# A 3x3 convolution by transformed tiles: from 2x2 outputs with 16 resident weight positions to 2x4 outputs with six streamed weight sets

## The chip, the cores and the metric

The kernel runs on one core of a Trainium2 chip, in one launch. The metric is device microseconds (us) of that core. A core has a matrix engine (TensorE, PE in the profile, with its weight loads apart as PEld), a vector engine (VectorE, DVE), an activation engine (ScalarE, ACT), a general engine (GpSimd, POOL), and a queue engine that only issues transfers here (SyncE, SP). Each engine works through its own instructions in order; semaphores tie them together. All arithmetic is in 32-bit floating point.

## What is computed

Two images of 256 channels and 64x64 pixels go through two layers, each added to its input. Layer 0 is an eight-head self-attention over all 4096 pixels. Layer 1 normalises by groups of channels, makes q, k and v by 1x1 products, and returns the mean of two branches: two block-wise attentions one after the other ("long range" over blocks, then "short range" inside blocks of 8x8, called `sr` below), and a 3x3 convolution over fixed mixtures of q, k and v:

```python
f_all = jnp.einsum('bidn,oi->bodn', jnp.concatenate([qh, kh, vh], 1), fc_w)
f_conv = f_all.transpose(0, 2, 1, 3).reshape(b, hd * KC * KC, h, w)
out_conv = lax.conv_general_dilated(f_conv, dep_w, (1, 1), ((1, 1), (1, 1)), feature_group_count=hd, dimension_numbers=('NCHW', 'OIHW', 'NCHW'))
return rate1 * out_att + rate2 * out_conv
...
x = x + _L0_conv_ref(_gn(x), L0_conv_qkv_w, L0_conv_qkv_b, 8)
x = x + _L1_conv_ref(_gn(x), ...)
```

Since everything before the convolution is linear, the kernel folds `conv1_w`, `conv2_w`, `conv3_w`, `fc_w` and `dep_w` into one dense 3x3 convolution with 256 input and 256 output channels. The change concerns how this convolution is done.

## The kernel before

**Stages.** Each image goes through five: statistics and projections of layer 0; its attention (TensorE, VectorE and ScalarE in an order written out by hand); `layer1_first`, which is the first attention of layer 1; and `layer1_second`, which holds the second attention and the convolution. Image 0 ends before image 1 begins, but for loads and statistics of image 1 that are worked in at the end (`following`). A second program, `general_layers`, is in the file for inputs whose softmax sums leave a safe range; it does not run here.

**Tiles.** A picture is held in eight tiles `xts[t]` of 128 partitions by 2 (channel halves) by 512 pixels (8 rows). `xp` is the normalised picture with a border of zeros. Working tiles come from one pool of 12 places (tag `w4`, 4 KB a partition): the hidden layers, v, z, `res` and others share it. A tile can be written when the last reader of the tile that had its place is done.

**The convolution before.** It uses the transform for 2x2 outputs from 4x4 inputs: 16 products stand for the 36 of the direct form. The picture is cut into four strips `s` of 16 rows, and each strip is worked in four steps, one for each column position `q`; a step handles all four row positions `r`. So an image has 16 steps, the two images 32. In one step:

- `conv_transform` (GpSimd): one operation makes `col` (1152 elements a partition) from strided columns of `xp` (L972), then four make the row positions, 512 elements each, in two `v` tiles (L976). It is called for the step after the one that is about to run.
- `conv_step`, products (TensorE, L986): 4 row positions x 2 output halves x 2 input halves, each 128x128 by 256 columns, into one PSUM tile `mm` of four banks, of which there is only one.
- `conv_step`, the way back: ScalarE copies one row position out of PSUM (L991), VectorE combines the others to two output rows in `z` (L992 to L995), and then adds or subtracts z into every second column of x: operations with the bias on 128 elements (L1007), the rest on 256 (L1011, L1013).

**Weights.** `conv_weights` (VectorE) folds them for one half `m` of the channels at a time: nine taps by twelve scaled additions (L905, L907), four row combinations, and from each row four column positions (L916 to L918), sent to DRAM in pieces of 128 KB by SyncE (L920). It runs while image 0's first attention tiles are worked. `fetch_conv_weights` loads all 16 positions (4 MB) to one place of 32 KB a partition (tag `vw`), which layer 0 uses for its values. For image 0 it also turns them on TensorE, 64 transposes through PSUM (L945), scales them on VectorE and ScalarE on the way back (L950, L948), and stores the turned ones to DRAM (L951) for image 1, which only loads them.

**The order in `layer1_second`.** It loops over eight tiles t of the second attention. Each has two branches of two layers of products with ScalarE evictions (`branch`, q then k: L1339, L1348), values, scores, a softmax on VectorE and ScalarE (L1084 to L1091), a transpose of it (L1096, `at`), copies (L1105) and the weighted sum (L1114). TensorE's order is that of the program text; the other engines' is set by a planner. `spots` says at which of three places in a tile a step is put: 0 between the branches, 1 between the softmax's start and its transpose, 2 at the tile's end. `images` says when the tiles of `xp` are made (`to_image`, ScalarE; before the loop also VectorE). `give(n)` adds the attention's result `res` to `xts[n]` and stores it once the strip that holds n is complete; `following` loads image 1 into the places of x that have become free.

```python
spots = {t: (0, 1, 2) for t in range(2, 7)} | {7: (0,)} if b == 0 else {
    t: (0, 1, 2) if t < 2 else (0, 1) for t in range(NT - 1)
}
```

Of the kernel before, what the change touches and what calls it, by code (L numbers as in the profile page):

```python
# [9 lines left out]
F32 = mybir.dt.float32  # L10
# [30 lines left out]
def direct_layers(ctx: ExitStack, tc: tile.TileContext, a: dict, out: bass.AP, bad: bass.AP):  # L41
# [805 lines left out]
    def conv_weights():  # L847
# [7 lines left out]
        prep, rest = place[:, :n_prep], place[:, n_prep : n_prep + 27 * C].rearrange("p (i c) -> p i c", c=C)  # L855
        wx, taps, new_rows = rest[:, 0:12], rest[:, 12:21], rest[:, 21:27]
        new_cols = rest[:, 0:8].rearrange("p (r j) c -> p r j c", j=2)
# [39 lines left out]
        for m in range(2):  # L897
# [16 lines left out]
            for r, row in enumerate((g[0], one, two, g[2])):  # L914
                one, two = new_cols[:, r, 0, :], new_cols[:, r, 1, :]
                nc.vector.tensor_add(one, row[:, 0, :], row[:, 2, :])  # L916
                nc.vector.tensor_sub(two, one, row[:, 1, :])
                kept["made"] = nc.vector.tensor_add(one, one, row[:, 1, :])  # L918
                for q, src in enumerate((row[:, 0, :], one, two, row[:, 2, :])):
                    nc.sync.dma_start(  # L920
                        out=wf_kept[:, :, 4 * r + q, m * P : (m + 1) * P], in_=src.rearrange("p (k c) -> p k c", k=KC)
                    )
# [6 lines left out]
    UW = 16  # L929
    wf_kept = dram.tile([P, KC, UW, C], F32, name="wf_kept")  # L930

    def fetch_conv_weights(b):

        wf = vpool.tile([P, KC, UW, C], F32, tag="vw", name=f"wf_{b}")
        for r in range(4):
            nc.sync.dma_start(out=wf[:, :, 4 * r : 4 * r + 4, :], in_=wf_kept[:, :, 4 * r : 4 * r + 4, :])
        if b > 0:
            return wf
        for pos in range(UW):
            r, q = divmod(pos, 4)  # L940
            pw = bank([P, KC, C], f"pw_{pos}")
            for k in range(KC):
                for m in range(2):
                    block = slice(m * P, (m + 1) * P)
                    nc.tensor.transpose(pw[:, k, block], wf[:, k, pos, block], ident)  # L945
            scale = (0.5 if r in (1, 2) else 1.0) * (0.5 if q in (1, 2) else 1.0)
            if pos % 2:
                nc.scalar.activation(wf[:, :, pos, :], pw, AF.Copy, scale=scale)  # L948
            else:
                nc.vector.tensor_scalar(wf[:, :, pos, :], pw, scale, None, ALU.mult)  # L950
        nc.sync.dma_start(out=wf_kept, in_=wf)  # L951
        return wf
# [6 lines left out]
    STRIP = 8 * (W // 2)  # L959

    def conv_transform(b, xp, s, q):

        def cols(d):
            return xp[:, :, 16 * s : 16 * s + 18, d : d + W - 1 : 2]

        def rows(d):
            return col[:, :, d : d + 15 : 2, :]

        terms = ((0, 2, False), (1, 2, True), (2, 1, False), (1, 3, False))
        col = cpool.tile([P, KC, 18, W // 2], F32, tag="col", name=f"col_{b}_{s}_{q}")  # L970
        one, two, plus = terms[q]
        (nc.gpsimd.tensor_add if plus else nc.gpsimd.tensor_sub)(col, cols(one), cols(two))  # L972
        v = [w4([P, 2, KC, STRIP], f"v_{b}_{s}_{q}_{n}") for n in range(2)]
        for r, (one, two, plus) in enumerate(terms):
            dst = v[r // 2][:, r % 2].rearrange("p k (i j) -> p k i j", j=W // 2)
            (nc.gpsimd.tensor_add if plus else nc.gpsimd.tensor_sub)(dst, rows(one), rows(two))  # L976
        return v

    def conv_step(b, xts, wf, v, s, q, pacc):


        mm = pacc.tile([P, 2, 4, STRIP], F32, tag="acc", name=f"mm_{b}_{s}_{q}")
        for r in range(4):
            for m in range(2):
                for k in range(KC):
                    nc.tensor.matmul(  # L986
                        mm[:, m, r, :], wf[:, k, 4 * r + q, m * P : (m + 1) * P], v[r // 2][:, r % 2, k, :],
                        start=k == 0, stop=k == KC - 1,
                    )
        z = w4([P, 2, 2, STRIP], f"z_{b}_{s}_{q}")  # L990
        nc.scalar.copy(z[:, 1], mm[:, :, 1, :])  # L991
        nc.vector.tensor_add(z[:, 0], z[:, 1], mm[:, :, 0, :])  # L992
        nc.vector.tensor_add(z[:, 0], z[:, 0], mm[:, :, 2, :])
        nc.vector.tensor_sub(z[:, 1], z[:, 1], mm[:, :, 2, :])
        nc.vector.tensor_sub(z[:, 1], z[:, 1], mm[:, :, 3, :])  # L995
        bias = kept["bias"][1]
        for half in range(2):
            xs = xts[2 * s + half].rearrange("p m (i r j c) -> p m i r j c", i=4, r=2, c=2)
            for r in range(2):
                zs = z[:, r, :, half * (STRIP // 2) : (half + 1) * (STRIP // 2)].rearrange(  # L1000
                    "p m (i j) -> p m i j", i=4
                )
                for c in range(2):
                    dst = xs[:, :, :, r, :, c]
                    if q - c == 0:
                        for m in range(2):
                            nc.vector.scalar_tensor_tensor(  # L1007
                                dst[:, m], zs[:, m], bias[:, m, 0:1], dst[:, m], ALU.add, ALU.add
                            )
                    elif (q, c) in ((1, 0), (2, 0)):  # L1010
                        nc.vector.tensor_add(dst, dst, zs)  # L1011
                    elif (q, c) in ((2, 1), (3, 1)):
                        nc.vector.tensor_sub(dst, dst, zs)  # L1013
# [255 lines left out]
    def layer1_second(b, xts, feats, mean, rstd, shift, pacc, following):  # L1269
# [8 lines left out]
        def to_image(t, both=False):  # L1278
# [10 lines left out]
        results = {}  # L1289
        turns = [divmod(n, 4) for n in range(4 * NT // 2)]  # L1290
# [5 lines left out]
        spots = {t: (0, 1, 2) for t in range(2, 7)} | {7: (0,)} if b == 0 else {  # L1296
            t: (0, 1, 2) if t < 2 else (0, 1) for t in range(NT - 1)
        }
        images = {1: range(5), 3: (5, 6), 4: (7,)} if b == 0 else {0: (3, 4), 1: (5,), 2: (6,), 3: (7,)}

        def conv():
            nonlocal done, wf
            if wf is None:
                wf = fetch_conv_weights(b)
            if done + 1 < len(turns):
                ahead[done + 1] = conv_transform(b, xp, *turns[done + 1])
            conv_step(b, xts, wf, ahead.pop(done), *turns[done], pacc)
            done += 1

        def give(n):  # L1310
            res = results.pop(n)
            halves = out[b, :, n * T : (n + 1) * T].rearrange("(k p) n -> p k n", p=P)
# [9 lines left out]

        if b:
            with tc.issue_after(kept["feats"].ins):
                for t in range(3):
                    to_image(t, True)
            ahead[0] = conv_transform(b, xp, *turns[0])
        pending, then = None, following()
        for t in range(NT):
# [25 lines left out]
            with tc.manual_schedule(engines={mybir.EngineType.PE}):  # L1355
# [9 lines left out]
                if b == 0 and t == NT - 1:  # L1365
                    for n in sorted(results):
                        give(n)
# [44 lines left out]
            for n in sorted(n for n in results if done >= 4 * (n // 2 + 1)):  # L1412
                give(n)
# [599 lines left out]
```

## Time and profile before

| what | us |
|---|---|
| three runs | 3078.77, 3077.24, 3078.86 (median 3078.77) |
| the profiled execution, its own time | 3078.72 |
| its span, first to last instruction | 3076.7 |
| `layer1_second`, image 0 | about 1256 to 1561 |
| `layer1_second`, image 1 | about 2784 to the end |
| products of the convolution (L986), busy | 227.6 |
| GpSimd, v of the transform (L976), busy | 165.4 |
| GpSimd, col of the transform (L972), busy | 69.5 |
| VectorE, updates of x (L1007; L1011; L1013) | 69.3; 28.9; 32.1 |

In the profile a line of instructions has its start, its length, the engine, the line of the program, the operation, what is written and read, the shape, and in brackets how long the engine had been idle before and what ended that. A matmul of 32-bit numbers appears as two, so a step's 16 products are counted as 32. The granted clock is TensorE's, 1.00 at full rate. Lines of transfers on SPq show when they were issued, not when they landed.

### The profile page before, as it was taken

To read this page: it belongs to the slowest core of one execution; us is meant where nothing else is said; L and a number is where in the kernel's file an instruction comes from. 1 tells how busy PE (TensorE), PEld (TensorE's weight loads), DVE (VectorE), ACT (ScalarE), POOL (GpSimd) and SP (SyncE) were. 2 spreads that over 40 slices of the span, in tenths; PEclk is the share of its full clock that TensorE was granted. 3 is DMA by queue.
4 is the path that set the end of the run, shared out by engine and by line. 5 is a ranking of instruction groups with operands and counts; after the bars stand their busy time and mean duration, and the time that the engine had idled before them with its cause. 6 is when DMAs were issued, how large, how long until landed. Compare 5 with 4: busy or idle time off the path is not lost. (4 is left out here: it accounts for less than half of the span.)

```text
span 3076.7 us, 63947 instructions
## 1 busy us (share of the span) xinstructions
PE 2991.9 (97%) x25129; PEld 1865.1 (61%) x25129; DVE 2455.0 (80%) x3122; ACT 2339.2 (76%) x3262; POOL 837.5 (27%) x923
## 2 busy tenths in 40 slices
PE   6999999999999999999989999999999999999998
PEld 3555556655556656577755556566555565576765
DVE  4598999999899989856556989989989899835543
ACT  2699999999999984622237999999999999734333
POOL 2032222322223230055301222222222222306440
PEclk9999999999999999999999999999999999999999
DMA  7979679787897661230159787897888976700000
GB/s 241 270 142 185 146 157 173 156 176 150 171 182 163 141 133 33 76 137 28 41 191 268 137 169 164 159 179 150 169 166 166 182 153 128 169 4 4 21 14 22
DMA packets 243795, 424.48 MB, mean 138 GB/s; under 512 B 99112, under 2 KB 109916, under 8 KB 241308
## 3 DMA queue, kind: packets, MB, share of 16 engines
q0 software_dynamic: 94992, 238.36, 40.3%
q1 hardware_dynamic: 147580, 181.68, 21.8%
q8 instruction: 199, 3.26, 0.4%
q14 instruction: 112, 0.92, 0.1%
q10 hardware_dynamic: 912, 0.27, 0.0%
HBM read 119.03 MB, written 68.39 MB: 61 GB/s over the span
## 5 line engine op out<-in xcount | busy, mean ns | idle before, releaser
L541 ACT ACTIVATE es<-ring 128x512 f32<-128x512 f32 (+2 forms) x1572 | 1204.1, 908 | 31.7 <-PE ring L535 23.7
L535 PE MATMUL ring<-q,k 128*128 128x512 f32 x4096 | 1085.0, 408 | 11.4 <-ACT v L541 6.2
L587 DVE TENSOR_TENSOR e<-e,es 128x1024 f32<-128x1024 f32 (+1 forms) x956 | 1035.7, 1145 | 23.7 <-ACT es L541 23.3
L535 PEld LDWEIGHTS ring<-q,k 128*128 128x128 f32 x4096 | 734.5, 188 | 383.2 <-ACT es L541 114.8
L541 ACT ACTIVATE v<-ring 128x512 f32<-128x512 f32 (+2 forms) x1024 | 781.2, 903 | 25.6 <-PE ring L535 12.9
L550 PE MATMUL av<-es,v 128*32 128x256 f32 (+1 forms) x9684 | 725.8, 389 | 0.0
L587 DVE TENSOR_TENSOR e<-e,v 128x1024 f32<-128x1024 f32 (+1 forms) x636 | 669.8, 1109 | 25.2 <-ACT v L541 24.2
L550 PE MATMUL av<-v 128*32 128x256 f32 (+1 forms) x6188 | 498.4, 389 | 0.0
L550 PEld LDWEIGHTS av<-es,v 128*32 128x32 f32 x9684 | 328.1, 110 | 265.9 <-issue 106.4
L550 PEld LDWEIGHTS av<-v 128*32 128x32 f32 x6188 | 221.5, 110 | 170.8 <-issue 72.3
L986 PE MATMUL mm<-v,wf 128*128 128x256 f32 x1024 | 227.6, 380 | 1.5 <-DVE z L995 1.5
L597 POOL DMA_DIRECT2D es<-es x118 | 100.7, 853 | 462.1 <-ACT es L541 392.4
L986 PEld LDWEIGHTS mm<-v,wf 128*128 128x128 f32 x1024 | 193.3, 190 | 36.8 <-issue 9.8
L976 POOL TENSOR_TENSOR v<-col 128x512 f32<-128x512 f32 x128 | 165.4, 1318 | 178.4 <-ACT rk_sr L1127 39.9
L991 ACT COPY z<-mm 128x512 f32<-128x512 f32 x32 | 18.7, 585 | 183.3 <-PE mm L986 183.3
L597 POOL DMA_DIRECT2D acc<-es x118 | 117.6, 1002 | 122.7 <-ACT es L541 43.0
L595 POOL DMA_DIRECT2D es<-es x20 | 11.4, 568 | 505.1 <-ACT es L541 414.8
L597 POOL DMA_DIRECT2D es<-v x72 | 61.3, 852 | 294.8 <-ACT v L541 288.7
L992 DVE TENSOR_TENSOR z<-z,mm 128x512 f32<-128x512 f32 x32 | 22.0, 687 | 139.7 <-ACT z L991 139.3
L597 POOL DMA_DIRECT2D v<-es x112 | 116.7, 1042 | 19.6 <-ACT es L541 10.2
L597 POOL DMA_DIRECT2D acc<-v x78 | 76.2, 977 | 75.9 <-ACT es L541 28.5
L972 POOL TENSOR_TENSOR col<-xp 128x1152 f32<-128x1152 f32 x32 | 69.5, 2173 | 62.4 <-DVE xp L1405 51.0
(252 smaller groups left out, 2685.8 us busy)
## 6 DMA issues: line engine op xcount, KB each, us to landing
acc<-es POOLq DMA_DIRECT2D x128, 512.0 KB, 6.4
acc<-v POOLq DMA_DIRECT2D x84, 512.0 KB, 6.1
es<-es POOLq DMA_DIRECT2D x138, 256.0 KB, 4.3
v<-es POOLq DMA_DIRECT2D x132, 256.0 KB, 5.2
k<-wk_halves SPq DMA_DIRECT2D x64, 512.0 KB
q<-wq_halves SPq DMA_DIRECT2D x256, 128.0 KB
v<-v POOLq DMA_DIRECT2D x90, 256.0 KB, 4.8
es<-v POOLq DMA_DIRECT2D x84, 256.0 KB, 3.9
```

What stands on the lines that cost most here:

```text
L535: touch(nc.tensor.matmul(sc[:, i, :], held["k", g // 2][:, j * P : (j + 1) * P], held["q", g, u // 2][:, u % 2, :], start=True, stop=True, ...
L541: nc.scalar.activation(dst, sc, AF.Exp, scale=SC0), set(range(at % BANKS, at % BANKS + m))
L550: note(nc.tensor.matmul(dst[HD0 * u : HD0 * u + HD0, n], lhs, rhs(u)[:, n], start=start, stop=stop))
L587: nc.vector.tensor_add(dst[:, s, :], dst[:, s, :], src)
L595: nc.gpsimd.dma_start(out=dst, in_=src)
L597: nc.gpsimd.dma_start(out=dst, in_=src, accum_op=ALU.add)
L972: (nc.gpsimd.tensor_add if plus else nc.gpsimd.tensor_sub)(col, cols(one), cols(two))
L976: (nc.gpsimd.tensor_add if plus else nc.gpsimd.tensor_sub)(dst, rows(one), rows(two))
L986: nc.tensor.matmul(mm[:, m, r, :], wf[:, k, 4 * r + q, m * P : (m + 1) * P], v[r // 2][:, r % 2, k, :], start=k == 0, stop=k == KC - 1,)
L991: nc.scalar.copy(z[:, 1], mm[:, :, 1, :])
L992: nc.vector.tensor_add(z[:, 0], z[:, 1], mm[:, :, 0, :])
```

## The change

The convolution's transform becomes one of two output rows by four columns: 4 row positions and six column positions, 24 products for 72.

- The picture is cut into two halves of 32 rows, each worked in six steps (`TURNS`: sets 0 to 5 for the upper half, 5 to 0 for the lower). A step again has 16 products of 256 columns. An image has 12 steps.
- `conv_transform` makes `col` (1088 elements) in four operations: two elementwise ones of GpSimd with a scaling by ScalarE between the first and the second, and a third of GpSimd. The four row operations remain, of 512 elements.
- The way back: z is laid out by picture tile; the bias is added by ScalarE where set 1 is copied out. VectorE then adds z, with a factor of 1, -1, 2, -2, 4, -4, 8 or -8, into every fourth column of each of the four tiles: four operations of 256 elements in sets 0 and 5, sixteen in the others.
- `conv_weights` makes six column positions from each row, with three scaled additions more, and sends 24 pieces for each half of the channels in place of 16.
- A class `ConvWeights` holds four of the six sets (1 MB each) in the same 32 KB a partition. Sets 4 and 5 are loaded after steps 0 and 1 of the upper half, sets 1 and 0 after the lower half's first two steps. For image 0, sets 0 to 3 are turned before the first step, 4 before the second, 5 before the third (96 transposes in all), and each set is stored.
- `spots` and `images` have new entries for 12 steps; before its loop image 1 makes five tiles of `xp` instead of three.
- Results: a tile of which the half is not complete has its attention result added to x (`add_result`) and is later stored from x itself (`give_summed`).

```diff
-        new_cols = rest[:, 0:8].rearrange("p (r j) c -> p r j c", j=2)
+        new_cols = [[rest[:, at, :] for at in range(4 * r, 4 * r + 4)] for r in range(3)]
+        new_cols.append([rest[:, at, :] for at in (15, 16, 17, 27)])
...
+                nc.vector.scalar_tensor_tensor(far[0], row[:, 2, :], 4.0, row[:, 0, :], ALU.mult, ALU.add)
+                nc.vector.scalar_tensor_tensor(far[1], row[:, 1, :], -2.0, far[0], ALU.mult, ALU.add)
+                kept["made"] = nc.vector.scalar_tensor_tensor(
+                    far[0], row[:, 1, :], 2.0, far[0], ALU.mult, ALU.add
+                )
+                for q, src in enumerate((row[:, 0, :], *near, *far, row[:, 2, :])):
...
+    TURNS = [(0, q) for q in range(NQ)] + [(1, q) for q in reversed(range(NQ))]
...
+        def fetch(self, q):
+            nc.sync.dma_start(out=self.wf[:, slot(q)], in_=wf_kept[:, q])
+            if q not in self.whole:
+                self.raw.append(q)
...
+        def used(self, n):
+
+            s, q = TURNS[n]
+            after = {(0, 0): 4, (0, 1): 5, (1, 5): 1, (1, 4): 0}.get((s, q))
+            if after is not None:
+                self.fetch(after)
...
+        (nc.gpsimd.tensor_add if plus else nc.gpsimd.tensor_sub)(col, cols(one), cols(two))
+        nc.scalar.activation(col, col, AF.Copy, scale=by)
+        (nc.gpsimd.tensor_add if third_plus else nc.gpsimd.tensor_sub)(col, col, cols(third))
+        nc.gpsimd.tensor_add(col, col, cols(fourth))
...
+    BY = ((1, 0, 0, 0), (1, 1, 1, 1), (1, -1, 1, -1), (1, 2, 4, 8), (1, -2, 4, -8), (0, 0, 0, 1))
...
+        for t in range(4):
+            xs = xts[4 * s + t].rearrange("p m (a j c) -> p m a j c", j=W // NC, c=NC)
+            zs = z[:, :, t, :].rearrange("p m (a j) -> p m a j", j=W // NC)
+            for c, by in enumerate(BY[q]):
+                dst = xs[:, :, :, :, c]
+                if abs(by) == 1:
+                    kept["given"] = (nc.vector.tensor_add if by > 0 else nc.vector.tensor_sub)(dst, dst, zs)
+                elif by:
+                    kept["given"] = nc.vector.scalar_tensor_tensor(dst, zs, float(by), dst, ALU.mult, ALU.add)
...
-        spots = {t: (0, 1, 2) for t in range(2, 7)} | {7: (0,)} if b == 0 else {
-            t: (0, 1, 2) if t < 2 else (0, 1) for t in range(NT - 1)
+        spots = {2: (0, 1), 3: (0, 1, 2), 4: (0, 1), 5: (0, 1), 6: (0, 1), 7: (0,)} if b == 0 else {
+            0: (1,), 1: (0, 1), 2: (0, 1), 3: (0, 1), 4: (0, 1), 5: (0, 1), 6: (0,)
         }
-        images = {1: range(5), 3: (5, 6), 4: (7,)} if b == 0 else {0: (3, 4), 1: (5,), 2: (6,), 3: (7,)}
+        images = {1: range(5), 3: (5, 6, 7)} if b == 0 else {0: (5, 6), 1: (7,)}
...
+            wf.turn()
             conv_step(b, xts, wf, ahead.pop(done), *turns[done], pacc)
+            wf.used(done)
...
+        def add_result(n, res):
+
+            for m in range(KC):
+                x = xts[n][:, m, :]
+                nc.vector.scalar_tensor_tensor(x, res[:, m, :], wts["rate1"], x, ALU.mult, ALU.add)
+            summed.append(n)
...
+        def give_summed():
+            for n in [n for n in summed if whole(n)]:
+                nc.sync.dma_start(out=of_image(n), in_=xts[n])
+                summed.remove(n)
...
-                for t in range(3):
+                for t in range(5):
                     to_image(t, True)
```

## The prediction

> **What bounds the kernel now.** I read the engines' shares first, then three windows.
>
> ```profile
> span 3076.7 us, 63947 instructions
> PE 2991.9 (97%) x25129; PEld 1865.1 (61%) x25129; DVE 2455.0 (80%) x3122; ACT 2339.2 (76%) x3262; POOL 837.5 (27%) x923
> ```
>
> ```profile
> 1256.00:1561.00 305.00, 291.22 (x1380) 205.04 (x1379) 196.29 (x405) 109.16 (x189) 121.61 (x85) 0.98 0.18 65
> 1340.00:1350.00 10.00, 7.51 (x34) 5.85 (x34) 8.82 (x23) 3.03 (x5) 1.02 (x2) 0.83 0.01 2
> 2784.00:3070.00 286.00, 280.73 (x1297) 193.92 (x1297) 133.99 (x267) 98.18 (x172) 117.58 (x80) 0.99 0.04 14
> ```
>
> The columns are stretch, length, then PE, PEld, DVE, ACT and POOL busy, the granted clock, DMA share and GB/s. The first and third are the two stages that hold the convolution (image 0, image 1). TensorE is the bound in both (95% and 98%); the others have room on average. The change can gain only by taking work from TensorE, and lose only where it makes TensorE wait. The middle row is such a wait, and TensorE's order of time around it shows the price of a step:
>
> ```profile
> 1315.70 7.15 PE L945 MATMUL pw<-ident,wf 128*128 128x128 f32 x64
> 1322.69 7.07 PE L986 MATMUL mm<-v,wf 128*128 128x256 f32 x32
> 1329.60 1.89 PE L1050 MATMUL pvs_sr<-wt_fv,feats 128*128 128x256 f32 x8
> 1331.42 1.15 PE L1068 MATMUL sp_sr<-rk_sr,rq_sr 128*64 128x64 f32 x32
> 1333.49 7.14 PE L986 MATMUL mm<-v,wf 128*128 128x256 f32 x32 [0.92 <-DVE z L995]
> 1343.12 0.44 PE L1096 MATMUL at_sr<-ident,e_sr 128*128 128x128 f32 x2 [2.49 <-DVE e_sr L1091]
> 1343.40 3.08 PE L1050 MATMUL pvs_sr<-wt_fv,feats 128*128 128x256 f32 x8
> ```
>
> What TensorE waited for there, on VectorE and GpSimd:
>
> ```profile
> 1333.26 7.45 DVE L1007 SCALAR_TENSOR_TENSOR x<-z,edges,x 128x128 f32<-128x128 f32 x7
> 1340.63 0.41 DVE L1084 TENSOR_REDUCE nm_sr<-sp_sr 128x4 f32<-128x256 f32 x1
> ```
>
> ```profile
> 1332.73 5.08 POOL L976 TENSOR_TENSOR v<-col 128x512 f32<-128x512 f32 x4 [5.65 <-PE sp_sr L1068]
> 1337.89 2.14 POOL L972 TENSOR_TENSOR col<-xp 128x1152 f32<-128x1152 f32 x1
> ```
>
> An update of x takes 0.34 us alone (median of L1007), but seven took 7.45 here, because each came through once per GpSimd instruction; the softmax's reduction L1084 stood behind them. This is the hazard of the change.
>
> **Part by part.**
>
> *Products.* A step is 16 products before and after, 256 columns each. It occupies TensorE from 1322.69 to 1329.60, 6.91 us. 32 steps become 24: 8 x 6.91 = **-55.3**.
>
> *Transposes.* 64 took 1315.70 to 1322.69, 0.109 each. 32 more: **+3.5**.
>
> *First step.* The bias leaves VectorE's eight half-size updates; four remain there. The wait above goes: 0.92 + 2.49, plus the slowed matmuls behind (3.08 for 1.89, and 2.57 for the 2.22 us of pc elsewhere, 1.5): **-4.9**.
>
> *GpSimd.* The rows:
>
> ```profile
> L976 POOL TENSOR_TENSOR v<-col 128x512 f32<-128x512 f32 x64 | 83.0, 1321 | 96.5 <-ACT rk_sr L1127 34.1 <-issue 15.0 <-DVE x L1013 14.1
> L972 POOL TENSOR_TENSOR col<-xp 128x1152 f32<-128x1152 f32 x16 | 34.6, 2163 | 10.2 <-ACT xp L1285 9.0
> L1007 DVE SCALAR_TENSOR_TENSOR x<-z,edges,x 128x128 f32<-128x128 f32 x64 | 32.1, 552 | 0.0
> L1011 DVE TENSOR_TENSOR x<-x,z 128x256 f32<-128x256 f32 x32 | 13.4, 418 | 0.0
> ```
>
> Before: 2.16 + 4 x 1.32 = 7.4 us a step. After: three column operations of 1088 elements, 2.08 by interpolating between these two rows, and four of 1.32, 11.5 us; the ScalarE scaling between them I put at 1.4 (between one and two of xp's 0.81 us for 512 elements). A chain of 13 us. A picture tile with two steps lasts 34.8 us (its first product at 2905.57, the next tile's at 2940.35), 17.4 a step, so it hides, with one transform worked ahead; only image 0's tile of three steps is near the limit. **0**; without that cover it costs what exceeds the step's interval.
>
> *VectorE.* Updates now: 128 x 0.344 + 128 x 0.418 = 97 us if alone, 130.3 measured (69.3 + 28.9 + 32.1), so 33 us of blocking, of which 4.9 reached TensorE. After: 72 updates of 256 elements per half picture, 288 in all, 192 adds at 0.418 and 96 scaled at 0.476 (L907's row) = 126 alone. z falls by 8 x 4 x 0.683 = 22. Average load is no bound, but the middle sets give 16 updates to a step, and GpSimd's busy share in the two convolution stretches (214 + 248 = 462 us) rises from 238/462 = 52% to 276/407 = 68%. Blocking scaled by both: 33 x 126/97 x 68/52 = 56; with the share 4.9/33 that reached TensorE, 8. That row has at most 12 updates in a step, so I take twice it, **+16**. Lower bound 0. Upper: in a tile with two such steps all 14 GpSimd instructions (23 us) let one update through each; the 18 other updates cost 7.7, two sums of results 1.5, z 5.5, the softmax and its copies 2.7, together 40.4 against 34.8, 5.6 us late, and 1.5 of slow clock; 16 such steps make 8 such pairs, 57. The wait is for the softmax; at_sr, pvs_sr and pc_sr are queued behind it on TensorE.
>
> *ScalarE's scaling* waits in ScalarE's queue for GpSimd's first subtraction. If placed early, the evictions behind it wait, and TensorE's branch products wait for those. Bounds: 0, and 2.1 + 1.4 less 1.0 of slack in a branch (half of its second layer's 3.6 us of products against an eviction of 0.78), 24 x 2.5 = 60. TensorE's waits for ScalarE in these stretches are a few us in total today, so nearer the low end: **+5**.
>
> *Weights of image 0.*
>
> ```profile
> 1295.65 9.07 SPq L920 DMA_DIRECT2D wf_kept<-prep  x11
> 1306.40 2.65 SPq L936 DMA_DIRECT2D wf<-wf_kept  x4
> ```
>
> Stores are issued 0.66 us apart; 17 instead of 11 come at the end (+4), and VectorE's 9 late extra operations at 0.40 pitch (3.6) lie beside that. The loads start near 1310.4, the transposes are due at 1315.70 and had no wait; I take **+3**, 0 to 12 (the first half's 8 extra stores stand before the loads of the second half).
>
> *Set 4* is loaded after step 0 and transposed before step 1. TensorE has 1.89 + 1.15 = 3.0 us between; today's four loads, issued from 1306.40, had all been used by 1322.69, at most 4.1 us each, and a lone load also has its start-up; I take 5. **+2**, 0 to 7. Set 5 has a whole tile's end and the next branch, 11 us, and image 1's later fetches four steps: 0. SP stands behind these waits, with only result stores and x loads.
>
> *Outputs* come from x itself, so image 1's last three x tiles load only after a store. Before, the stage's end has 16 statistics in VectorE from 1542.31 to 1554.95, which cover most: **+2**, 0 to 6. Image 1's five tiles of picture instead of three are covered since its first step moves one branch and the scores later. Sums of results replace the gives one for one: 0.
>
> Sum: 3076.7 - 55.3 + 3.5 - 4.9 + 16 + 5 + 3 + 2 + 2 = 3048.0. The profiled execution's own time, 3078.72, is 2.0 above its span, and the median 3078.77 equals it: **3050**.
>
> [...] The trace has a 0.83 clock after 2.49 us idle. [...]
> [...]
>
> **Rivals.** (A) The above: 3050, 3030 to 3070, chance 0.48.
> (B) VectorE, ScalarE and the loads hide it all, as TensorE's 98% speaks for: 3078.7 - 55.3 + 3.5 - 4.9 = 3022, chance 0.15. Against it: the wait at 1343.
> (C) The blocking decides: slower from 5.6 us per pair of heavy steps, as (3076.7 - 3032.0)/8; at the upper bound 7.1 it gives 3050 + 57 - 16 = **3091**, slower. For it: 7.45 us for seven updates. Against: 56 of today's 64 L1011 updates met no GpSimd instruction. 0.20.
> (D) ScalarE's queue blocks in each transform: 3050 + 60 - 5 = 3105. Nothing like it in the trace, since no ScalarE instruction there waits for GpSimd. 0.08.
> (E) The weights come late at every place: +12 + 7 + 6 for 7: 3068. 0.09.
>
> **Numbers.** 0.2% (6 us) is about what a measurement here can tell. Faster: A 0.44, B 0.15, E 0.07, 0.66. Same: 0.10 from the edges of A, E and C. Slower: C 0.16, D 0.08, 0.24. Range 3022 to 3094, B to C.
>
> **What would show it.** 768 products of 256 columns in place of 1024 by the trace's count; GpSimd near 11.5 us a step; L1007's successors above 0.42 where GpSimd runs; TensorE's waits at at_sr (my +16), at the branch products (ScalarE), at pw (weights). I am wrong if TensorE's idle time in the two stages grows beyond 50 us, or does not grow at all.

## The result, and the profile after

The changed kernel takes 3148.52 us (median of four runs, 3147.52 to 3150.63) beside 3078.82 (3077.24 to 3079.41) for the kernel before: a ratio of 1.0223, 95% interval 1.021 to 1.0236. It is **slower by 69.7 us**. The prediction said 3050 and gave 3022 to 3094, so it has the wrong sign and the time lies outside its range. One execution of experiment 5 below took 9620.31 us, for 3119.40 to 3121.59 of its three others, and is left out of that experiment's median.

The engines' shares of the profiled execution after:

```profile
span 3148.7 us, 63534 instructions
PE 2969.5 (94%) x24905; PEld 1831.1 (58%) x24905; DVE 2598.6 (83%) x3152; ACT 2360.0 (75%) x3284; POOL 952.0 (30%) x931
```

TensorE has 22.4 us less work (2991.9 before), and the span is 72.0 us longer, so some 94 us of new idle time stand against it. It lies in the two stages. In the names of the profile, `phq_sr` and `phk_sr` are the first-layer products of the q and the k branch in PSUM, `hq_sr` and `hk_sr` ScalarE's evictions of them (copies out of PSUM), `prq_sr`, `prk_sr`, `rq_sr` and `rk_sr` the same of the second layer; `e_sr` is the softmax, `at_sr` its transpose, `bd` the copy of that, `pc_sr` the weighted sum, `pw` the turning of the weights, and `mm` the accumulator of the convolution's products. These are the stretches of image 0 and image 1, each taken from the first `phq_sr` product to the stage's end, and 20 us inside the first (columns as before: stretch, length, PE, PEld, DVE, ACT, POOL busy, granted clock, DMA share, GB/s):

```profile
1262.16:1607.90 345.74, 280.96 (x1268) 190.24 (x1269) 267.56 (x418) 118.51 (x199) 179.64 (x89) 0.91 0.22 78
2829.35:3148.70 319.35, 265.63 (x1169) 173.88 (x1169) 198.15 (x267) 105.74 (x178) 174.87 (x84) 0.93 0.08 27
1436.00:1456.00 20.00, 5.22 (x12) 2.70 (x12) 19.89 (x15) 1.93 (x3) 14.74 (x7) 0.66 0.00 1
```

The stages last 345.7 and 319.4 us, for 302.3 and 292.6 before from and to the same instructions. TensorE's gaps between matmuls, added up in the trace's records (without the last wait of image 0's stage, 3.1 us in both kernels), are 107.1 us in the two, for 12.0 before, and the clock is granted at half for 110.5 us, for 21.8. The clock is the second loss: products and transposes alone were to take 51.8 us from TensorE's work, but only 22.4 us are gone, since the matmuls behind the gaps run slowly (the eight of `prq_sr` behind the longest wait for ScalarE, shown below, took 5.91 us for 3.60 where nothing was late). So the account is -22.4 + 95.1 = +72.7, for 72.0 measured.

What TensorE waited for, from the waits of the whole span (total, times, longest):

```profile
PE prq_sr L1413 <- ACT hq_sr L1172: 41.3, 12, 10.4
...
PE at_sr L1141 <- DVE e_sr L1136: 17.2, 7, 4.6
PE mm L1027 <- DVE z L1049: 14.8, 1, 14.8
PE prk_sr L1413 <- ACT hk_sr L1172: 7.5, 2, 7.0
PE pc_sr L1159 <- ACT rq_sr L1172: 7.2, 1, 7.2
PE pw L970 <- DVE e_sr L1131: 5.1, 1, 5.1
```

Before, the waits for `hq_sr` were not there, and those for `e_sr` were these:

```profile
PE at_sr L1096 <- DVE e_sr L1091: 3.6, 2, 2.5
```

More than half of the new waits are for ScalarE (some 60 of the 95 us), which has more room than TensorE and VectorE; so one has to ask what ScalarE waited for:

```profile
ACT x L1065 <- DVE x L1056: 66.9, 18, 20.9
...
ACT col L1008 <- POOL col L1007: 52.1, 9, 12.6
```

These are the border corrections behind the late updates of x, and the new scaling behind GpSimd's first column operation. The groups of the convolution's own instructions (busy us, mean ns, idle before):

```profile
L1027 PE MATMUL mm<-v,wf 128*128 128x256 f32 x768 | 176.0, 389 | 14.8 <-DVE z L1049 14.8
L1056 DVE TENSOR_TENSOR x<-x,z 128x256 f32<-128x256 f32 x192 | 170.3, 981 | 0.8
...
L1015 POOL TENSOR_TENSOR v<-col 128x512 f32<-128x512 f32 x96 | 136.4, 1451 | 1.9
L1058 DVE SCALAR_TENSOR_TENSOR x<-z,x 128x256 f32<-128x256 f32 x96 | 102.5, 1129 | 0.0
L1009 POOL TENSOR_TENSOR col<-col,xp 128x1088 f32<-128x1088 f32 x24 | 76.0, 3167 | 128.4 <-ACT col L1008 128.4
L1010 POOL TENSOR_TENSOR col<-col,xp 128x1088 f32<-128x1088 f32 x24 | 73.3, 3056 | 1.9
...
L1007 POOL TENSOR_TENSOR col<-xp 128x1088 f32<-128x1088 f32 x24 | 64.5, 2688 | 67.3 <-DVE xp L1469 55.0 <-ACT xp L1330 10.6
```

The updates of x before:

```profile
L1007 DVE SCALAR_TENSOR_TENSOR x<-z,edges,x 128x128 f32<-128x128 f32 x128 | 62.9, 542 | 0.0
L1013 DVE TENSOR_TENSOR x<-x,z 128x256 f32<-128x256 f32 x64 | 30.8, 502 | 0.0
L1011 DVE TENSOR_TENSOR x<-x,z 128x256 f32<-128x256 f32 x64 | 28.9, 451 | 0.0
```

The products fell as predicted, 1024 to 768. The updates of x keep VectorE busy for 170.3 + 102.5 = 272.8 us, for 62.9 + 30.8 + 28.9 = 122.6. (Neighbouring updates overlap a little. By the sum of their lengths, which is what the table ahead of the prediction gives with 130.3, they take 296.8 us.) GpSimd's four kinds take 136.4 + 76.0 + 73.3 + 64.5 = 350.2 us, 14.6 us a step.

**The longest wait, read closely.** VectorE, then GpSimd, then TensorE, in order of time:

```profile
1435.40 8.40 DVE L1058 SCALAR_TENSOR_TENSOR x<-z,x 128x256 f32<-128x256 f32 x3
1443.71 1.70 DVE L1056 TENSOR_TENSOR x<-x,z 128x256 f32<-128x256 f32 x1
1445.26 6.20 DVE L1058 SCALAR_TENSOR_TENSOR x<-z,x 128x256 f32<-128x256 f32 x3
1451.36 0.68 DVE L1046 TENSOR_TENSOR z<-z,mm 128x512 f32<-128x512 f32 x1
```

```profile
1434.63 3.71 POOL L1009 TENSOR_TENSOR col<-col,xp 128x1088 f32<-128x1088 f32 x1 [1.22 <-ACT col L1008]
1438.41 3.31 POOL L1010 TENSOR_TENSOR col<-col,xp 128x1088 f32<-128x1088 f32 x1
1441.80 6.23 POOL L1015 TENSOR_TENSOR v<-col 128x512 f32<-128x512 f32 x4
1448.11 2.86 POOL L1007 TENSOR_TENSOR col<-xp 128x1088 f32<-128x1088 f32 x1
```

```profile
1454.23 2.04 PE L1027 MATMUL mm<-v,wf 128*128 128x256 f32 x4 [14.78 <-DVE z L1049]
```

Seven updates take the 16 us of seven GpSimd instructions, one for each. The four z operations, the last of which releases the accumulator, stand behind them, and the next step's product waited 14.78 us. The row of 1436 to 1456 above shows the price: VectorE 19.89 of 20.00 busy, TensorE 5.22, clock 0.66. The z operations themselves, which have one input in PSUM, all take 0.67 to 0.69 us, also beside GpSimd.

The other kind of wait, in ScalarE's order of time, and TensorE's row:

```profile
1303.27 0.42 ACT L1132 ACTIVATE e_sr<-e_sr 128x256 f32<-128x256 f32 x1 [0.23 <-DVE e_sr L1131]
1313.24 1.11 ACT L1008 ACTIVATE col<-col 128x1088 f32<-128x1088 f32 x1 [9.56 <-POOL col L1007]
1314.26 1.43 ACT L1172 ACTIVATE hq_sr<-phq_sr,vecs 128x512 f32<-128x512 f32 x2
```

```profile
1315.07 5.91 PE L1413 MATMUL prq_sr<-hq_sr,wt_fq 128*128 128x512 f32 x8 [10.44 <-ACT hq_sr L1172]
```

The scaling waited 9.56 us for GpSimd, and the evictions of `hq_sr`, whose products were complete about 1304.6, stood behind it: TensorE's wait of 10.4 us. There GpSimd itself began late, at 1310.32, since the clearing of the picture's border (L1469) is put behind VectorE's preparation of the weights. The kernel before had that order too (its GpSimd began at 1303.21), but nothing on ScalarE stood behind GpSimd.

### The profile page after: what moved, and what is told of

The parts are those of the page before. It is cut to its first block, busy times and chain, and to the rows that moved or that the text cites. A ratio compares the mean times of both kernels' runs of the same rounds, so it can differ in the third digit from the quotient of the medians.

```text
span 3148.7 us, 63534 instructions
## 1 busy us (share of the span) xinstructions
PE 2969.5 (94%) x24905; PEld 1831.1 (58%) x24905; DVE 2598.6 (83%) x3152; ACT 2360.0 (75%) x3284; POOL 952.0 (30%) x931
## 4 chain that ended last, share of the span: by engine, by line
PE 46%; DVE 9%; ACT 2%; POOL 1%; DMA 1%; issue 1%; ACTq 0%; POOLq 0%; DVEq 0%
PE ring L535 16%; PE av L550 14%; PE mm L1027 4%; DVE x L1056 3%; DVE x L1058 3%; PE prq_sr L1413 1%; PE p_wk L406 1%; PE py L1211 1%; PE pvs_lr L1095 1%; PE pv L429 1%; PE p_wq L406 1%; PE prk_sr L1413 1%; PE pvs_sr L1095 1%; PE phk_sr L1404 1%; PE ring L550 1%
## 5 line engine op out<-in xcount | busy, mean ns | idle before, releaser
L1027 PE MATMUL mm<-v,wf 128*128 128x256 f32 x768 | 176.0, 389 | 14.8 <-DVE z L1049 14.8
L1027 PEld LDWEIGHTS mm<-v,wf 128*128 128x128 f32 x768 | 148.6, 195 | 41.2 <-issue 20.4
L1056 DVE TENSOR_TENSOR x<-x,z 128x256 f32<-128x256 f32 x192 | 170.3, 981 | 0.8
L1015 POOL TENSOR_TENSOR v<-col 128x512 f32<-128x512 f32 x96 | 136.4, 1451 | 1.9
L597 POOL DMA_DIRECT2D v<-es x112 | 115.4, 1030 | 17.2 <-ACT es L541 9.0
L1009 POOL TENSOR_TENSOR col<-col,xp 128x1088 f32<-128x1088 f32 x24 | 76.0, 3167 | 128.4 <-ACT col L1008 128.4
L1413 PE MATMUL prq_sr<-hq_sr,wt_fq 128*128 128x512 f32 x128 | 71.8, 705 | 41.4 <-ACT hq_sr L1172 41.3
L1058 DVE SCALAR_TENSOR_TENSOR x<-z,x 128x256 f32<-128x256 f32 x96 | 102.5, 1129 | 0.0
```

The lines of the kernel that those rows point to most:

```text
L597: nc.gpsimd.dma_start(out=dst, in_=src, accum_op=ALU.add)
L1009: (nc.gpsimd.tensor_add if third_plus else nc.gpsimd.tensor_sub)(col, col, cols(third))
L1027: nc.tensor.matmul(mm[:, r, m, :], wf.wf[:, slot(q), k, r, m * P : (m + 1) * P], v[r // 2][:, r % 2, k, :], start=k == 0, stop=k == KC - 1,)
L1056: kept["given"] = (nc.vector.tensor_add if by > 0 else nc.vector.tensor_sub)(dst, dst, zs)
L1058: kept["given"] = nc.vector.scalar_tensor_tensor(dst, zs, float(by), dst, ALU.mult, ALU.add)
L1413: nc.tensor.matmul(pr[m], wts[two][:, k, m * P : (m + 1) * P], hid[:, k, :], start=k == 0, stop=k == KC - 1)
```

## The experiments

Two theories at first. **L**: VectorE's updates are late (each update excludes, and is excluded by, GpSimd's instructions, and costs more alone than I had put down), and everything else is late because of them. **Q**: ScalarE's queue is the cause, by the scaling that waits for GpSimd and the border corrections that wait for updates. All edits are to the changed kernel.

**1. The scaling on GpSimd.**

```
-        nc.scalar.activation(col, col, AF.Copy, scale=by)
+        nc.gpsimd.tensor_scalar(col, col, by, None, ALU.mult)
```

> The changed kernel, with the scaling of col done by GpSimd instead of ScalarE, so that no ScalarE instruction of the convolution waits for GpSimd. Theory Q (ScalarE's queue: evictions stand behind the scaling): the waits of TensorE for the evictions of t=2 of image 0 and t=0 of image 1 (10.4, 7.2, 4.3 and 7.0 us) go, and some slow clock with them: 3105 to 3120. Theory L (VectorE's updates and GpSimd's operations exclude each other, and the rest follows from late updates): GpSimd gets 24 operations more, so 3148 or up to 20 more.

Measured: 3143.72 us, ratio to the kernel before 1.0208 (1.0178 to 1.0238). The waits changed place:

```profile
PE at_sr L1141 <- DVE e_sr L1136: 42.7, 6, 15.5
...
PE prq_sr L1413 <- ACT hq_sr L1172: 28.5, 9, 9.5
```

The waits for the softmax (VectorE) rose from 17.2 to 42.7 as those for ScalarE fell. Q alone falls.

**2. The border corrections left out.**

```
-            for tt in ((), (0, 1))[t] if b == 0 and t < 2 else (t,):
-                conv_edges(xts, tt)
```

> The changed kernel without the border corrections of the bias (conv_edges left out, so border pixels lack them). Theory Q: ScalarE's border operations wait for late updates of x and hold up evictions (5.0, 5.9, 8.9 and 3.4 us at hq); without them 3115 to 3125. Theory L in its strict form (TensorE waits for VectorE itself): within 5 us of 3148.

Measured: 3138.62 us, 1.0191 (1.0162 to 1.0221), 10 us less: between the two expectations, nearer L's.

**3. Both at once.**

> Both of the former: GpSimd scales, and the border corrections are left out. Theory Q: nothing in ScalarE's queue waits for GpSimd or for updates of x any more, so most of the 60 us of waits for evictions go: 3070 to 3090. Theory L strict: 3140 to 3170.

Measured: 3142.17 us, 1.0203 (1.0173 to 1.0233). No wait of note for `hq_sr` is left; those for `e_sr` are 61.2 us, and the time is within 7 us of the changed kernel's. ScalarE's queue was mostly where the lateness showed, not what made it: L.

**4. A third of the updates.** Of sets 0 to 4 only the first column that has a factor is updated: 96 updates for 288.

```
-            for c, by in enumerate(BY[q]):
+            for c, by in enumerate(BY[q][:1] if q < 5 else BY[q]):
```

> The changed kernel with one column of updates a step (96 updates of x in place of 288; three of four columns do not get sets 1 to 4). Theory L: VectorE and GpSimd no longer contend, waits at the softmax and at z and late border operations go: 3070 to 3085. Theory Q with the scaling alone as the cause: the four waits behind the scaling stay (29 us and slow clock), 3110 to 3125.

Measured: 3092.95 us, 1.0045 (1.0025 to 1.0065): 55.6 us less, between the two ranges and nearer L's. L gets most of it, but the waits for `hq_sr` keep 26.0 us (longest 10.4), so the scaling has a price of its own, which experiment 1 could not show while VectorE was late.

**5. z in PSUM.** Does L come from the exclusion (L1 below) or from the price of an update alone (L2)? The two last z operations write to the accumulator's first two banks, whose products are used up by then; the updates then have one SBUF input.

```
-        nc.vector.tensor_add(z0, z0, products(2))
         nc.vector.tensor_sub(z1, z1, products(2))
-        nc.vector.tensor_sub(z1, z1, products(3))
+        zp = mm[:, 0:2].rearrange("p r m s -> p (r m s)").rearrange("p (m t s) -> p m t s", m=2, t=4)
+        of_row = zp.rearrange("p m t (i r j) -> p (m t i) r j", r=2, j=W // NC)
+        nc.vector.tensor_add(of_row[:, :, 0, :], z0, products(2))
+        nc.vector.tensor_sub(of_row[:, :, 1, :], z1, products(3))
...
-            zs = z[:, :, t, :].rearrange("p m (a j) -> p m a j", j=W // NC)
+            zs = zp[:, :, t, :].rearrange("p m (a j) -> p m a j", j=W // NC)
```

> The last two of the four z operations write z into the accumulator's first two banks in PSUM in place of SBUF, so each of the 288 updates of x has one SBUF input and not two; nothing else is changed. Theory L1 (the updates are late because an operation of VectorE with two SBUF inputs and GpSimd's operations exclude each other): no update is over 1 us any more, their mean is 0.63 to 0.75 us (981 and 1129 ns in the changed kernel), their sum 180 to 215 us for 272.8, and the time falls by 35 to 70 us, to 3080 to 3113. Rival L2 (the price of every fourth column alone, 0.63 for 0.418, makes them late): the sum falls little in what counts and the time stays within 12 us of 3148. Rival Q (ScalarE's scaling in the queue): the waits for hq_sr keep their 41 us and the time stays over 3120. A cost that may come in: the accumulator's banks stay taken until the last update, so a product may wait for them.

Measured: 3120.46 us, 1.0133 (1.0113 to 1.0154), 28.1 us less. The updates, and the new wait for them:

```profile
L1058 DVE TENSOR_TENSOR x<-x,mm 128x256 f32<-128x256 f32 x192 | 106.6, 627 | 0.8
...
L1060 DVE SCALAR_TENSOR_TENSOR x<-mm,x 128x256 f32<-128x256 f32 x96 | 53.9, 634 | 0.0
```

```profile
PE mm L1027 <- DVE x L1060: 22.3, 7, 7.0
PE prq_sr L1415 <- ACT hq_sr L1174: 15.6, 6, 10.4
PE mm L1027 <- DVE x L1058: 10.6, 4, 2.9
```

Not one of the 288 updates is over 0.72 us (81 were over 1 us), though GpSimd works beside them as before. So L1's mechanism stands, and the waits for `hq_sr` fall from 41.3 to 15.6 us. The time, though, lies over L1's range, and Q's "over 3120" came true: the gain is less than L1 expected, because the accumulator is now held until the last update (22.3 + 10.6 = 32.9 us of product waits) and the scaling is still in ScalarE's queue.

**6. Updates to contiguous places.** The same number of the same size, but to a contiguous quarter of the row block.

```
-                dst = xs[:, :, :, :, c]
+                dst = xts[4 * s + t][:, :, P * c : P * (c + 1)].rearrange("p m (a j) -> p m a j", j=W // NC)
```

> Each update goes to a contiguous quarter of its row block in place of every fourth column; the sums that land in x are other ones, count and sizes are the same, and both inputs stay in SBUF. L2 (stride's price): an update alone falls from 0.63 to about 0.42 us or below, the sum of the updates by 60 us or more, and the time by 30 to 55 us, to 3095 to 3120. L1 (exclusion): the updates beside GpSimd's operations keep 1.6 to 3.4 us, the sum stays over 215 us, and the time falls by less than 20 us.

Measured: 3117.96 us, 1.0127 (1.0107 to 1.0147), 30.6 us less. The median update is 0.42 us for 0.64, the price that I had predicted for the strided one, but 71 are still over 1 us:

```profile
L1056 DVE TENSOR_TENSOR x<-x,z 128x256 f32<-128x256 f32 x192 | 127.0, 721 | 0.8
L1058 DVE SCALAR_TENSOR_TENSOR x<-z,x 128x256 f32<-128x256 f32 x96 | 79.3, 878 | 0.0
```

The time lies in L2's range and not in L1's, while the 71 late updates are what L1 expected. Both halves of L are real: the stride has a price, and the exclusion is there without it (222.8 us by the sum of the lengths, where 288 x 0.418 would be 120.4).

**7. z in PSUM and the scaling on GpSimd** (edits 5 and 1).

> z in PSUM as in the run beside it, and the 24 scalings of the column tile on GpSimd in place of ScalarE (some 3.1 us each there, 1.1 on ScalarE). With the updates free of GpSimd, the scaling is the one part of the transform left in ScalarE's queue. Theory Q' (once VectorE is in time, TensorE's waits for ScalarE's evictions behind a scaling that waits for GpSimd decide): 15 to 35 us below the run with z in PSUM alone, 3055 to 3085. Theory L1 alone (ScalarE's queue was late only because the border corrections waited for late updates): within 8 us of the run with z in PSUM alone. If GpSimd becomes the bound with 3 us more a step (some 16.5 us of a step of 25), products wait for v and the time rises.

Measured: 3091.71 us, 1.0038 (1.0024 to 1.0052): 28.8 us under z in PSUM alone, where the same edit brought 4.8 us to the changed kernel. The drop lies inside the range of Q', the time itself above it, and Q' holds: with VectorE in time, the scaling in ScalarE's queue is the next cost. Product waits for the accumulator stay at 33.2 us.

**8. z in PSUM and sums of pairs.** The z of a pair's first set is kept; at the second, sum and difference are made once, and x gets 16 updates for 32. The main lines:

```
...
+        if opens:
+            return
+        if pair is not None:
+            (nc.vector.tensor_sub)(*((dp, kept["pair"], zp) if q in (2, 4) else (dp, zp, kept["pair"])))
+            nc.vector.tensor_add(zp, zp, kept["pair"])
...
```

> z in PSUM, and fewer updates: the z of sets 1 and 3 (first strip; 2 and 4 in the second) is kept in SBUF, at the other set of the pair the sum and the difference of the two are made once in PSUM (two operations of 1024 elements, some 1.1 us each by the 1024-element ratio to the 512-element z operations' 0.69), and x gets 16 updates for the pair in place of 32: 160 updates for 288. The working pool has 11 places for 12 to make room. Theory L (VectorE's work behind the products sets the time): the updates sum to 100 to 125 us, 15 to 40 us below z in PSUM alone, 3050 to 3085. Theory Q' (with exclusion gone the rest is ScalarE's scaling): within 8 us of z in PSUM alone. If the place less in the pool holds up hid or e tiles, the time rises.

Measured: 3117.78 us, 1.0126 (1.0109 to 1.0143), within 4 us of z in PSUM alone, although VectorE has some 60 us less to do (128 updates of 0.63 less, 16 sums of 1.23 more). By itself this doesn't show that VectorE's amount of work no longer counts, since the products still wait for the accumulator behind the updates (15.9 + 5.1 us; 15.8 more have no named cause) and three waits behind the scaling stay (10.4, 7.8, 7.6). Experiment 10 asks it again.

**9. The accumulator in two tiles**, beside edits 5 and 1: rows 2 and 3 of the products come first and lie in a tile that no z is written to.

```
-        mm = pacc.tile([P, 4, 2, STRIP], F32, tag="acc", name=f"mm_{b}_{s}_{q}")
-        for r in range(4):
+        low, high = [pacc.tile([P, 2, 2, STRIP], F32, tag=f"acc{n}", name=f"mm{n}_{b}_{s}_{q}") for n in (0, 1)]
+        mm = (low[:, 0], low[:, 1], high[:, 0], high[:, 1])
+        for r in (2, 3, 1, 0):
...
```

> z in PSUM and the scaling on GpSimd as in the run at 3091.7 us, and the accumulator in two tiles of two banks, (rows 0, 1) and (rows 2, 3); the products of rows 2 and 3 are issued first, then 1, then 0. z lies in the first tile, so the second is free after the z operations. There the products waited for the last update of x some 33 us in the two stages (20.9 and 12.3; single waits 2.5 to 7.1 us). Theory L (what is left is the accumulator held by updates): the first eight products take 3.5 us meanwhile, so each of the some 14 waits loses up to 3.5 us; the product waits fall to 5 to 12 us in all, and the time to 3055 to 3075, under the kernel before. Theory G (GpSimd's chain, now 16.8 us a step, or VectorE's work itself sets the time): the waits move to v or to VectorE's other work, and the time stays within 10 us of 3091.

Measured: **3044.77 us**, ratio to the kernel before **0.9891 (0.9874 to 0.9907)**, 47 us under experiment 7 and under its expected range: more than the 33.2 us of the waits, since the clock recovers too (26.7 us below full speed for 58.8). The split and the order of the products were not tried apart. This version beats both kernels, by 33 and 104 us. Its two stages and what is left of the waits:

```profile
1259.55:1551.65 292.10, 268.51 (x1268) 183.42 (x1269) 209.39 (x419) 106.83 (x187) 208.51 (x101) 0.97 0.26 93
2775.44:3043.60 268.16, 253.38 (x1169) 169.30 (x1169) 151.24 (x267) 94.58 (x166) 205.03 (x96) 0.98 0.09 32
```

```profile
PE pc_sr L1162 <- DVE bd L1153: 7.6, 4, 4.6
...
PE at_sr L1144 <- DVE e_sr L1139: 4.3, 2, 2.6
PE mm L1028 <- POOL v L1015: 3.6, 4, 1.5
...
PE prq_sr L1416 <- ACT hq_sr L1175: 2.8, 5, 1.4
...
PE mm L1028 <- DVE x L1061: 1.9, 1, 1.9
```

**10. The same with sums of pairs** (edit 8; the updates from the second tile go first).

> As the run beside it, and the sums and differences of a pair of sets made once (160 updates for 288, 16 additions or subtractions of 1024 elements, 11 places in the working pool for 12); the updates from the second tile go first. Theory L: at a pair's first set no update follows and at its second the second tile is free after half of them, so the product waits fall under 8 us in all: 3040 to 3070, and 5 to 20 us below the split accumulator alone. Theory G: within 8 us of the split accumulator alone, the rest being GpSimd's chain or the fixed waits. If the place less in the pool costs, it is above it.

Measured: 3045.08 us, 0.9895 (0.9878 to 0.9911), the same as experiment 9. Fewer updates bring nothing where they are in time; what the place less in the working pool may have cost is not separated.

**11 and 12. Experiment 9 with one part undone**: z in SBUF again, and the scaling on ScalarE again.

> The version of 3044.8 us with one part undone: z lies in SBUF again (scaling on GpSimd and the split accumulator stay), so that the updates have two SBUF inputs again. Theory L1 (exclusion between VectorE's updates and GpSimd is the cost that carries the rest): many updates take 1.6 to 3.4 us again, their sum is 240 to 290 us for 185, and the time is 3115 to 3148, next to the 3143.7 of the scaling on GpSimd alone. Rival (the split and the order of the products alone bring the gain): 3045 to 3075.

> The version of 3044.8 us with the other part undone: the scaling is on ScalarE again (z in PSUM and the split accumulator stay). Theory Q' (the scaling that waits for GpSimd in ScalarE's queue still holds up evictions that TensorE waits for): waits for hq_sr, hk_sr and rq_sr of 20 to 35 us come back, 3065 to 3085. Rival (with the updates in time and the accumulator free, ScalarE has slack for it): within 8 us, 3040 to 3053.

Measured: 3147.35 us, 1.0215 (1.0198 to 1.0233) with z in SBUF, and 3074.15, 0.9986 (0.9977 to 0.9996) with the scaling on ScalarE. With z in SBUF, 90 updates are over 1 us, and the waits are nearly those of experiment 1 (43.0 us for `e_sr` and 27.9 for `hq_sr`, there 42.7 and 28.5):

```profile
L1057 DVE TENSOR_TENSOR x<-x,z 128x256 f32<-128x256 f32 x192 | 196.3, 1116 | 0.8
L1059 DVE SCALAR_TENSOR_TENSOR x<-z,x 128x256 f32<-128x256 f32 x96 | 91.0, 1012 | 0.0
```

With the scaling on ScalarE:

```profile
PE prq_sr L1416 <- ACT hq_sr L1175: 15.5, 6, 10.4
PE prk_sr L1416 <- ACT hk_sr L1175: 9.8, 2, 9.3
PE pc_sr L1162 <- ACT rq_sr L1175: 7.5, 1, 7.5
```

So from the best version, z in SBUF costs 102.6 us, the undivided accumulator with the old order of products 46.9 (experiment 7), and the scaling on ScalarE 29.4. They do not add up to the 103.7 us between it and the changed kernel, because each wait hides the others: with z in SBUF the split and the move of the scaling bring 1.2 us together (3147.35 for 3148.52).

## Why the prediction was wrong

**The failed step is *VectorE*, "+16" with "Upper: ... 57".** The mechanism named there is the one that decided: one update let through per GpSimd instruction, and waits behind it on TensorE. With the rest in time it costs 102.6 us (experiment 11 beside 9), not 16. Already in the trace before, five of the seven updates that took 7.45 us were let through so; the two behind GpSimd's last instruction took 0.34 each. The sizes were too small in three places.

- The update alone was put at 0.418, from a row that writes every second column, and 0.476 scaled. Every fourth column costs 0.63 for both; experiment 6 finds 0.42 where the places are contiguous. By their durations 288 updates are 181 us if alone, not 126.
- GpSimd's column operations were put at 2.08 by interpolation between rows of every second column and contiguous ones. They take about 2.6 (2.2 to 2.3 in set 3), 3.04 and 3.04 when VectorE leaves them alone, and a step's seven operations 14.6 us as measured beside VectorE, not 11.5. They are the very instructions that an update waits for. The picture was read with a step of 8 bytes before (2.14 for 1152 elements) and is read with one of 16 now, but that the step of the reads makes the price is not shown: the two operations of 3.04 also write where they read, and so does the scaling on GpSimd in experiment 9, which took 2.97 alone on contiguous data.
- The formula of the upper bound, with these sizes, gives 29.2 for the 14 GpSimd instructions, 11.3 for the 18 other updates and the same 9.7 us for the rest: 50.2 us against the tile's 34.8, 15.4 late and not 5.6. Eight such pairs with 1.5 us of slow clock each are 135 us, not 57. The measured growth of TensorE's gaps, 95.1, lies inside that bound and outside the stated one.

The prediction also let only the softmax wait for the updates. The trace shows three more: the z operations of the next step (14.8 us at once), the turning of set 4 (5.1 us, behind four updates that took 7.67), and ScalarE's border corrections, with the evictions behind them (66.9 us of ScalarE's waits).

**The second is *ScalarE's scaling*, "+5", bounds 0 to 60.** I took the low end because TensorE waited little for ScalarE before; but before, no ScalarE instruction waited for GpSimd, which rival D's own text says, so that row told nothing. Measured with the rest in time: 29.4 us, not in 24 small parts but in three waits of 10.4, 7.5 and 9.3 us. All three fall where GpSimd makes a stage's first two transforms one behind the other and ScalarE reaches the scaling before GpSimd is so far.

**Rival C had the mechanism**, with 0.20, but priced it at 3091 by the same small sizes; D's 3105 was nearer in number. Both were at work, and the prediction treated them as alternatives: taking D's scaling away alone brings 4.8 us (experiment 1), C's exclusion alone 28.1 (5), and both together 56.8 (7).

**What held.** Products: 768 for 1024; busy 227.6 before, 171.4 in experiment 9, where the clock is nearly whole, 56.2 less for the 55.3 predicted. Transposes: 7.2 to 11.2 there, +4.0 for +3.5. *GpSimd*, "0": TensorE waits for v nowhere in the changed kernel, and 3.6 us in experiment 9, with one more GpSimd operation of 3.16 us a step. Set 4: one wait of 2.3 us for its load, for +2 (that a load has a start-up shows in the kernel before, where loads of 128 KB took 5.3 and 5.5 us from issue to landing and those of 256 KB to `wv` 5.6). Weights of image 0: their loads are issued 51.4 us after the stage's start for 47.1, but the first transposes waited for none, so 0 for +3. Outputs: the statistics at the stage's end wait 3.1 and 3.1 us for 2.8 and 3.1, so about 0 for +2. Rival B's 3022 asked for every cost to be hidden; experiment 9 comes within 23 us of it, with 15.6 us more gaps than before.

**What else did not.** *First step*, -4.9: the wait for the softmax went, but the 5.1 us of set 4 above came in its place, behind the same step's updates. And the sums of results were put at 0, "one for one". VectorE is done with the weights later (it clears the picture's border 47.8 us after the stage's start, for 43.6), then makes two sums that took 3.69 us beside GpSimd's first column operation, and the copy `bd` comes behind them. In the changed kernel this is hidden behind the wait for the scaling; where the scaling is on GpSimd it is a wait of 4.6 us, the longest that is left in experiment 9.

The sign to be wrong by, idle time of TensorE that grows by more than 50 us, is there: 95.1.

The sum's 16 was scaled from the two engines' loads over both stages, and that average was a mistake: the updates over 1 us don't spread evenly. In the changed kernel 13 of one step's sixteen were, those behind which the products waited 14.78 us, and none in six of the 24 steps. The runs show on which updates it falls: none of 288 was over 0.72 us with one input in PSUM (experiment 5), 90 were over 1 us with both in SBUF (experiment 11).

## What to carry to other kernels

Where VectorE and GpSimd work side by side, look at which of VectorE's operations read two inputs from SBUF, and try to have one of them in PSUM; here that was worth 102.6 us, and once it was done and the accumulator split, 128 updates less brought nothing. A change of stride can be a change of price: do not carry a row of every second element (0.418 us) over to every fourth (0.63). And an instruction that waits for a slow engine holds up all that stands behind it in its own engine's queue; it is paid for in a few long waits (here three of 24, of 10.4, 9.3 and 7.5 us), not at the mean. When several such waits overlap, mend them together before judging one of them useless.

## What was not expected of the hardware

- VectorE's updates of float data cost more at a step of four elements: 256 elements 0.63 us, for 0.418 at a step of two (kernel before) and 0.42 contiguous (experiment 6). GpSimd's 1088 elements took 2.2 to 2.7 us with two inputs of step four, 3.04 with one of step four and one contiguous, updated in place, and 2.97 for the scaling of contiguous data in place (experiment 9); 1152 elements from two inputs of step two took 2.14 before.
- With GpSimd's column operations beside them, single updates of 0.63 us took up to 3.5 us: about the whole length of the other engine's instruction. GpSimd lost less: its v operations took 1.28 us alone and 1.45 in the mean of the changed kernel.
- Reading z from PSUM instead of SBUF cost an update nothing: 0.627 and 0.634 us in the mean (experiment 5) for 0.639 and 0.626 where no GpSimd instruction ran beside it (changed kernel).
